# Running sums of exponentials over eight key tiles instead of two or four, in a fused attention and FFN block

## The chip, the cores and the metric

The kernel runs on one core of a Trainium2 chip. The metric is the device time of one execution in microseconds (us); before the change it is 3277.49 us, the median of three runs from 3269.68 to 3278.75. Five engines work side by side, each through its own queue in program order: TensorE (PE in the profile; its weight loads are PEld), VectorE (DVE), ScalarE (ACT), GpSimd (POOL) and SyncE (SP), which issues most of the transfers. ScalarE's queue issues some too.

## The reference

One pre-norm transformer block in float32, on x of 2 x 1024 x 1024 (batch, tokens, features), with 32 heads of 32 features and an FFN of 2752 hidden units:

```python
def attention(x):
    qkv = (x @ attn_qkvw + attn_qkvb).reshape(B, S, 3, HEADS, hd)
    q, k, v = (transpose(qkv[:, :, i], (0, 2, 1, 3)) for i in range(3))
    probs = softmax(einsum('bhqd,bhkd->bhqk', q, k) / sqrt(hd))
    ctx = transpose(einsum('bhqk,bhkd->bhqd', probs, v), (0, 2, 1, 3))
    return ctx.reshape(B, S, H) @ attn_ow + attn_ob

x = x + attention(layernorm(x))
h = layernorm(x)
x = x + (silu(h @ W_gate.T) * (h @ W_up.T)) @ W_down.T
```

## The kernel before

**Blocks, phases and units.** The tokens are taken in four blocks of 512 queries (two batches of two). A phase is the attention of one block; it has 16 units, and a unit is two heads against all 1024 keys, in NT = 8 key tiles of 128. So there are 64 units, of which the first 16 (phase 0) stand among the projections of batch 0, and those of phases 1 to 3 largely among the output projection and FFN of the block before. The FFN of the last block has no attention beside it. The FFN products are of Strassen's kind, with sums of weights prepared by GpSimd during phase 0 (`weight_sum_steps`, L1148).

**A unit, step by step.** `scores` (L500) takes two key tiles at once: eight 32-row products (recorded as 8 instructions for a pair of tiles) into two PSUM buffers; ScalarE copies each to a tile p of 128x1024 in SBUF (L528), VectorE keeps a running maximum over the tiles (L525). After the last pair the maximum over the keys is found and negated, goes out to HBM and comes back as a tile m, spread over all partitions. `less_maximum` (L579) adds m to each p, on GpSimd (in phase 0 every fourth tile on VectorE), and puts the exponential (L590, ScalarE) and the sum (L601) off to later. `values` (L610) multiplies p by v into one PSUM bank `acc`: 16 records in four column groups for each key tile, and 8 more records with a tile of ones wherever `summed(kt)` says that p holds a sum, which gives the denominators.

**Sums in place of separate products.** If p1 is replaced by p0 + p1, then p0 v0 + p1 v1 = p0 (v0 - v1) + (p0 + p1) v1, so the values stay right when v0 becomes v0 - v1, and the ones need to be multiplied with the sum only. `add` (L601) makes the sums, `differences` (L593) changes v. In phases 1 to 3 the sums go over two tiles (adds for kt = 1, 3, 5, 7; GpSimd does 1 and 5, VectorE 3 and 7), so ones are multiplied four times per unit; in phase 0 they go over four tiles (six adds by VectorE), so ones are multiplied twice.

**What sets the order.** All instructions are emitted by hand. An `Emitter` keeps a planned clock, which advances by a cost for each TensorE step (855 ns for a product of 512 columns, MM4). It merges two lists: `fill` (projections, FFN) and `paced` (attention), whose beats are spread evenly over the costs of the list; there is one beat for each key tile n of all units. `em.later(delay, fn)` puts a step off by so many ns of the planned clock. A step with `needs` waits in its list until another one has given that name. In each round n of `attention_steps` (L650) come, in this order: q and k loads of the next unit, the load of v (L493, at kt = 6), the scores (at even n), `less_maximum` of tile n - 11, and every fourth round a run of four `values`, for tiles up to n - 14. The tiles p lie in a ring of 19 (`RING`, L165), vals in two buffers.

**Block changes.** When a block's attention is complete, its ctx is loaded, multiplied by the reciprocals of the sums (`prep_ctx`, L697; the products are on GpSimd, L730, and wait for the tile rec), and the next output projection begins (L752), with bias sums on GpSimd (L774).

Of the kernel before, what the change touches and what calls it, by code (L numbers as in the profile page):

```python
# [12 lines left out]
ALU = mybir.AluOpType  # L13
# [117 lines left out]
def preln_block_kernel(  # L131
# [31 lines left out]
    LAG = 3  # L163
    RUN = 4
    RING = NT + LAG + RUN + 4  # L165

    const = ctx.enter_context(tc.tile_pool(name="const", bufs=1))
    lin = ctx.enter_context(tc.tile_pool(name="lin", bufs=1))
# [295 lines left out]
    class Unit:  # L464
# [35 lines left out]
        def scores(self, i):  # L500

            kts = (2 * i, 2 * i + 1)
            ps = [
                psum.tile([P, S], F32, tag="s", bufs=2, name=f"s_{self.name}_{kt}") for kt in kts
            ]
            for a in range(2):
                for h in range(2):
                    rows = slice((2 * a + h) * HD, (2 * a + h + 1) * HD)
                    nc.tensor.matmul(  # L509
                        ps[a][:, h * NH : (h + 1) * NH],  # L510
                        self.k[rows, i * P : (i + 1) * P],
                        self.q[rows, :],
                        start=True,
                        stop=True,
                    )


            for kt in kts:
                self.p[kt] = Pt(f"p_{self.name}_{kt}")

            def largest(kt, s):
                if kt == 1:
                    self.top = att.tile([P, S], F32, tag="top", bufs=1, name=f"top_{self.name}")
                if kt > 0:
                    nc.vector.tensor_tensor(self.top, s, self.p[0] if kt == 1 else self.top, ALU.max)  # L525

            def keep(kt, s):
                nc.scalar.copy(self.p[kt], s)  # L528

            if i == 0:  # L530
                keep(0, ps[0])
                em.later(2600.0, lambda: largest(1, ps[1]))
            else:
                largest(kts[0], ps[0])
                em.later(1600.0, lambda: keep(kts[0], ps[0]))
                em.later(1700.0, lambda: largest(kts[1], ps[1]))
            em.later(3300.0 if i > 0 else 4200.0, lambda: keep(kts[1], ps[1]))
            if kts[1] == NT - 1:
                self.maximum()
# [39 lines left out]
        def less_maximum(self, kt):  # L579
            p = self.p[kt]  # L580
            eng = nc.vector if self.phase == 0 and kt % 4 == 3 else nc.gpsimd
            eng.tensor_tensor(p, p, self.m, ALU.add)  # L582
            em.later(3500.0, lambda: self.exponential(kt))
            if kt % 2 == 1:
                twice = self.phase == 0 and kt % 4 == 3
                em.later(8100.0, lambda: self.add(kt, 1), None if twice else ("added", self.n, kt))
                if twice:
                    em.later(9900.0, lambda: self.add(kt, 2), ("added", self.n, kt))

        def exponential(self, kt):  # L590
            nc.scalar.activation(self.p[kt], self.p[kt], AF.Exp, scale=SCALE)  # L591

        def differences(self):  # L593

            v = self.v.rearrange("p (i a) n -> p i a n", a=2)
            nc.gpsimd.tensor_tensor(v[:, :, 0, :], v[:, :, 0, :], v[:, :, 1, :], ALU.subtract)
            if self.phase == 0:
                v = self.v.rearrange("p (i a) n -> p i a n", a=4)
                nc.gpsimd.tensor_tensor(v[:, :, 1, :], v[:, :, 1, :], v[:, :, 3, :], ALU.subtract)

        def add(self, kt, back):  # L601


            eng = nc.vector if self.phase == 0 or kt % RUN == RUN - 1 else nc.gpsimd
            eng.tensor_tensor(self.p[kt], self.p[kt], self.p[kt - back], ALU.add)  # L605

        def summed(self, kt):
            return kt % (4 if self.phase == 0 else 2) == (3 if self.phase == 0 else 1)

        def values(self, kt):  # L610

# [38 lines left out]
    def attention_steps(cuts):  # L650
# [10 lines left out]

        for i in range(2):
            load_step(0, i)
        for n in range(total + NT + LAG + 3):
            if n in cuts:
                q = Steps()
                lists.append(q)
# [1 line left out]
            if n < total:  # L669
                if kt == 1 or kt == 3:  # L670
                    load_step(k + 1, kt // 2)
                if n == 0:
                    q.add(lambda: em.later(9000.0, lambda: None, ("first",)))
                    q.add(lambda: None, needs=("first",))
                if kt == NT - 2:
                    q.add(units[k].load_v, needs=("v", units[k].b, units[k].hf))
            if n < total and kt % 2 == 0:
                q.add(lambda k=k, i=kt // 2: units[k].scores(i), MM4, beat=True)
            else:
                q.add(lambda: None, beat=True)  # L680
            k, kt = divmod(n - NT - LAG, NT)
            if 0 <= k < len(units):
                if kt == 0:
                    q.add(units[k].differences)
                q.add(lambda k=k, kt=kt: units[k].less_maximum(kt), needs=("max", k))
            k, kt = divmod(n - NT - LAG - 3, NT)
            if 0 <= k < len(units) and kt % RUN == RUN - 1:
                q.add(lambda: None, needs=("added", k, kt))
                for v in range(kt - RUN + 1, kt + 1):
                    cost = MM4 / 2 * (1 + units[k].summed(v))  # L690
                    q.add(lambda k=k, v=v: units[k].values(v), cost)
        return lists


# [660 lines left out]
```

## Time and profile before

| | before |
|---|---|
| median of three runs | 3277.49 us (3269.68 to 3278.75) |
| the profiled execution | 3264.24 us, span 3262.5 us, TensorE clock 0.996 |
| first and last score maximum of a unit (L567) | 123 us, 2712 us |
| first and last copy of a finished unit (L639) | 200.6 us, 2776.9 us |
| ScalarE busy: exponentials (L591), copies of scores (L528) | 533.2 us, 516.7 us |
| GpSimd busy: differences of v (L596, L599) | 56.3 us, 10.1 us |
| SP waiting for values before it loads v (L495) | 241.5 us, 57 times |

The units follow one another about every 41 us. A row of groups reads: line, engine, operation, what it writes and reads, shapes and count; then busy time in us and the mean of one in ns; then the engine's idle time just ahead of these instructions and what ended most of it. A float32 product is recorded as two instructions. A row of stages has the window, its length, and busy us and instruction counts of PE, PEld, DVE, ACT and POOL, followed by the granted clock, the share of the DMA engines and GB/s. A row of the timeline has start, length, engine, line and operation, with several like instructions merged.

### The profile page before, as it was taken

The numbers are of one execution on the slowest core, as the hardware profiler recorded it, in microseconds if no ns is written. First come the engines' busy times: TensorE is split into PE (matmuls) and PEld (weight loads), VectorE is DVE, ScalarE is ACT, GpSimd is POOL, SyncE is SP. The second block draws the span as 40 slices with busy tenths as digits, with TensorE's granted clock in tenths as the row PEclk, the third lists the DMA queues.
The fourth block names the chain that finished last, engine by engine and source line by source line (L and its number), as shares of the span: only waits on it lengthen the run. The fifth ranks groups of instructions, "written<-read, shape, count | busy, mean of one in ns | idle before, by whom it ended". The sixth has DMA issues, their size and how long they took to land.

```text
span 3262.5 us, 43853 instructions
## 1 busy us (share of the span) xinstructions
PE 3206.8 (98%) x16256; PEld 1792.5 (55%) x16256; DVE 1999.2 (61%) x2733; ACT 1432.7 (44%) x1570; POOL 1767.8 (54%) x871
## 2 busy tenths in 40 slices
PE   8999999999999999999999999999999999999999
PEld 4444444444346565663466555634666567477775
DVE  2266676666356677667766777676677774344334
ACT  2244554444456555554565555545655554010000
POOL 0267766776676555667766665667756555200000
PEclk9999999999999999999999999999999999999999
DMA  4566666655435444446344444463444444544442
GB/s 155 170 183 197 219 197 205 194 173 170 140 107 149 146 147 148 146 149 205 104 142 146 146 143 143 143 201 101 142 147 149 144 139 139 178 156 152 154 153 96
DMA packets 337828, 507.31 MB, mean 155 GB/s; under 512 B 105424, under 2 KB 122064, under 8 KB 337616
## 3 DMA queue, kind: packets, MB, share of 16 engines
q1 hardware_dynamic: 281424, 405.91, 39.9%
q10 hardware_dynamic: 56192, 98.60, 9.8%
q8 instruction: 130, 2.13, 0.3%
q14 instruction: 82, 0.67, 0.1%
HBM read 429.14 MB, written 75.24 MB: 155 GB/s over the span
## 4 chain that ended last, share of the span: by engine, by line
PE 86%; DVE 6%; DMA 3%; POOL 2%; issue 1%; ACT 1%; SPq 0%; ACTq 0%; POOLq 0%; DVEq 0%
PE p L924 31%; PE pq L370 11%; PE pd L1073 11%; PE acc L620 9%; PE s L509 7%; PE pvv L432 7%; PE po L782 7%; DVE top L525 1%; DVE x L1086 1%; POOL p L582 1%; DMA ctx<-dctx 1%; DMA rec<-drec 1%; PE pg L968 1%; PE pd L1000 1%; DVE p L605 1%
## 5 line engine op out<-in xcount | busy, mean ns | idle before, releaser
L582 POOL TENSOR_TENSOR p<-p,m 128x1024 f32<-128x1024 f32 x480 | 1193.3, 2508 | 11.5 <-DVE top L525 8.4
L528 ACT COPY p<-s 128x1024 f32<-128x1024 f32 x512 | 516.7, 1011 | 840.3 <-DVE top L525 642.1
L591 ACT ACTIVATE p<-p 128x1024 f32<-128x1024 f32 x512 | 533.2, 1057 | 270.0 <-POOL p L582 246.2
L525 DVE TENSOR_TENSOR top<-s,top 128x1024 f32<-128x1024 f32 x384 | 468.0, 1219 | 275.1 <-PE s L509 266.1
L924 PE MATMUL p<-sum,m 128*128 128x256 f32 x2688 | 616.7, 383 | 4.1 <-DVE sum L906 3.6
L924 PEld LDWEIGHTS p<-sum,m 128*128 128x128 f32 x2688 | 503.0, 190 | 126.5 <-issue 45.7
L605 POOL TENSOR_TENSOR p<-p,p 128x1024 f32<-128x1024 f32 x96 | 227.1, 2366 | 629.7 <-ACT p L591 595.6
L924 PE MATMUL p<-xn2T,m 128*128 128x256 f32 x2016 | 471.1, 383 | 5.2 <-DVE sum L833 2.4
L370 PE MATMUL pq<-xnT,wqk 128*128 128x512 f32 x1024 | 463.2, 601 | 0.0
L1073 PE MATMUL pd<-wp,h 128*128 128x512 f32 x960 | 438.0, 602 | 10.3 <-DVE x L1086 9.9
L924 PEld LDWEIGHTS p<-xn2T,m 128*128 128x128 f32 x2016 | 376.7, 190 | 104.4 <-issue 47.9
L605 DVE TENSOR_TENSOR p<-p,p 128x1024 f32<-128x1024 f32 x192 | 335.7, 1748 | 135.5 <-ACT p L591 134.8
L370 PEld LDWEIGHTS pq<-xnT,wqk 128*128 128x128 f32 x1024 | 188.2, 190 | 255.9 <-issue 252.7
L1073 PEld LDWEIGHTS pd<-wp,h 128*128 128x128 f32 x960 | 177.1, 190 | 248.1 <-issue 200.0
L509 PE MATMUL s<-q,k 32*128 32x512 f32 x2048 | 302.2, 643 | 10.6 <-ACT p L528 10.5
L1086 DVE TENSOR_TENSOR x<-pd,x 128x512 f32<-128x512 f32 x360 | 236.7, 681 | 71.1 <-PE pd L1073 70.6
L620 PE MATMUL acc<-p,vals 128*32 128x256 f32 x4096 | 266.2, 382 | 5.5 <-DVE p L605 5.4
L1186 POOL TENSOR_TENSOR ws<-raw 128x512 f32<-128x512 f32 x62 | 89.3, 1440 | 300.5 <-DMA raw<-in_w_gu 188.9
L432 PE MATMUL pvv<-wv,xnT 128*128 128x512 f32 x512 | 234.3, 603 | 2.4 <-ACT xnT L266 2.4
L782 PE MATMUL po<-wo,ctx 128*128 128x512 f32 x512 | 234.4, 608 | 0.0
L620 PEld LDWEIGHTS acc<-p,vals 128*32 128x32 f32 x4096 | 119.5, 109 | 147.3 <-issue 71.3
L952 ACT ACTIVATE gate<-gate 128x512 f32<-128x512 f32 x84 | 52.9, 630 | 278.0 <-DVE gate L951 277.4
(94 smaller groups left out, 2476.9 us busy)
## 6 DMA issues: line engine op xcount, KB each, us to landing
m<-dws SPq DMA_DIRECT2D x336, 256.0 KB
m<-in_w_gu SPq DMA_DIRECT2D x252, 256.0 KB
wp<-ddn SPq DMA_DIRECT2D x160, 256.0 KB
m<-d SPq DMA_DIRECT2D x64, 512.0 KB
wp<-in_w_dn SPq DMA_DIRECT2D x120, 256.0 KB
raw<-in_w_gu ACTq DMA_DIRECT2D x84, 256.0 KB
dws<-ws ACTq DMA_DIRECT2D x84, 256.0 KB
x<-in_x SPq DMA_DIRECT2D x32, 512.0 KB
```

The lines of the kernel that those rows point to most:

```text
L370: nc.tensor.matmul(ps, wqk[b, g, w, hk][:, k, :], xnT[b, s][:, kc, :], start=(kc == 0), stop=(kc == KC - 1),)
L432: nc.tensor.matmul(st["ps"], xnT[b, t // TB][:, kc, (t % TB) * P : (t % TB + 1) * P], st["w"][kc], start=(kc == 0), stop=(kc == KC - 1),)
L509: nc.tensor.matmul(ps[a][:, h * NH : (h + 1) * NH], self.k[rows, i * P : (i + 1) * P], self.q[rows, :], start=True, stop=True,)
L525: nc.vector.tensor_tensor(self.top, s, self.p[0] if kt == 1 else self.top, ALU.max)
L528: nc.scalar.copy(self.p[kt], s)
L582: eng.tensor_tensor(p, p, self.m, ALU.add)
L591: nc.scalar.activation(self.p[kt], self.p[kt], AF.Exp, scale=SCALE)
L605: eng.tensor_tensor(self.p[kt], self.p[kt], self.p[kt - back], ALU.add)
L620: nc.tensor.matmul(self.acc[j * HD : (j + 1) * HD, c : c + NQ], w(h), self.p[kt][:, q0 : q0 + NQ], start=start, stop=stop, skip_group_chec ...
L782: nc.tensor.matmul(st["ps"], ctxT[b, blk][:, g, t * P : (t + 1) * P], st["w"][hf, g], start=(g == 0), stop=(g == G - 1),)
L924: nc.tensor.matmul(ps, mats[c, n][:, kc, :], rhs, start=(kc == 0), stop=(kc == hk - 1),)
L1073: nc.tensor.matmul(st["pd"], lefts[n](pi)[:, j, t * P : (t + 1) * P], st["wp", pi, n, j], start=(j == 0), stop=(j == PART // 2 - 1),)
```

## The change

Four things change.

1. **Sums over all eight tiles, in all phases** (`SUMS = 8`). p of tile kt becomes the sum of the exponentials of tiles 0 to kt, in seven adds one after another. `summed` is true for kt = 7 alone, so ones are multiplied once per unit. `differences` makes seven instructions, v of tile a less v of tile a + 1.
2. **Who adds.** In phase 0 VectorE does all seven; in phases 1 to 3 VectorE does kt = 3, 5 and 7, GpSimd kt = 1, 2, 4 and 6. The adds are put off by 8100 ns (phase 0), 11000 ns (GpSimd) or 12500 ns (VectorE) of the planned clock after the tile's `less_maximum`, and by 500 ns again for as long as the add before has not been emitted.
3. **Values one tile later.** A run of four values is for tiles up to n - 15 instead of n - 14, and is emitted directly after the scores of the round and ahead of `less_maximum`, where before it came last in a round without scores. v is loaded one tile later (kt = 7).
4. **Tiles p are claimed when the scores are copied**, not when the score products are emitted. The ring keeps its 19 tiles.

```diff
+    SUMS = 8
...
-            for kt in kts:
-                self.p[kt] = Pt(f"p_{self.name}_{kt}")
...
             def keep(kt, s):
+
+                self.p[kt] = Pt(f"p_{self.name}_{kt}")
                 nc.scalar.copy(self.p[kt], s)
...
-            if kt % 2 == 1:
-                twice = self.phase == 0 and kt % 4 == 3
-                em.later(8100.0, lambda: self.add(kt, 1), None if twice else ("added", self.n, kt))
-                if twice:
-                    em.later(9900.0, lambda: self.add(kt, 2), ("added", self.n, kt))
+            if kt % SUMS > 0:
+
+                vec = self.phase == 0 or (kt > 1 and kt % 2 == 1)
+                delay = 8100.0 if self.phase == 0 else 12500.0 if vec else 11000.0
+                eng = nc.vector if vec else nc.gpsimd
+                em.later(delay, lambda: self.add(kt, eng))
...
-            v = self.v.rearrange("p (i a) n -> p i a n", a=2)
-            nc.gpsimd.tensor_tensor(v[:, :, 0, :], v[:, :, 0, :], v[:, :, 1, :], ALU.subtract)
-            if self.phase == 0:
-                v = self.v.rearrange("p (i a) n -> p i a n", a=4)
-                nc.gpsimd.tensor_tensor(v[:, :, 1, :], v[:, :, 1, :], v[:, :, 3, :], ALU.subtract)
-
-        def add(self, kt, back):
-
-
-            eng = nc.vector if self.phase == 0 or kt % RUN == RUN - 1 else nc.gpsimd
-            eng.tensor_tensor(self.p[kt], self.p[kt], self.p[kt - back], ALU.add)
+            v = self.v.rearrange("p (i a) n -> p i a n", a=SUMS)
+            for a in range(SUMS - 1):
+                nc.gpsimd.tensor_tensor(v[:, :, a, :], v[:, :, a, :], v[:, :, a + 1, :], ALU.subtract)
+
+        def add(self, kt, eng):
+
+            if kt % SUMS > 1 and ("added", self.n, kt - 1) not in em.done:
+                em.later(500.0, lambda: self.add(kt, eng))
+                return
+            eng.tensor_tensor(self.p[kt], self.p[kt], self.p[kt - 1], ALU.add)
+            em.done.add(("added", self.n, kt))

         def summed(self, kt):
-            return kt % (4 if self.phase == 0 else 2) == (3 if self.phase == 0 else 1)
+            return kt % SUMS == SUMS - 1
...
-        for n in range(total + NT + LAG + 3):
+        for n in range(total + NT + LAG + 4):
...
-                if kt == NT - 2:
+                if kt == NT - 1:
                     q.add(units[k].load_v, needs=("v", units[k].b, units[k].hf))
...
+
+            k, kt = divmod(n - NT - LAG - 4, NT)
+            if 0 <= k < len(units) and kt % RUN == RUN - 1:
+                q.add(lambda: None, needs=("added", k, kt))
+                for v in range(kt - RUN + 1, kt + 1):
+                    cost = MM4 / 2 * (1 + units[k].summed(v))
+                    q.add(lambda k=k, v=v: units[k].values(v), cost)
             k, kt = divmod(n - NT - LAG, NT)
             if 0 <= k < len(units):
                 if kt == 0:
                     q.add(units[k].differences)
                 q.add(lambda k=k, kt=kt: units[k].less_maximum(kt), needs=("max", k))
-            k, kt = divmod(n - NT - LAG - 3, NT)
-            if 0 <= k < len(units) and kt % RUN == RUN - 1:
-                q.add(lambda: None, needs=("added", k, kt))
-                for v in range(kt - RUN + 1, kt + 1):
-                    cost = MM4 / 2 * (1 + units[k].summed(v))
-                    q.add(lambda k=k, v=v: units[k].values(v), cost)
```

## The prediction

> **What bounds the kernel now.** I read the engine shares first, then the groups by line and shape, then the busy time by stage, then single moments on the timeline.
>
> ```profile
> PE 3206.8 (98%) x16256; PEld 1792.5 (55%) x16256; DVE 1999.2 (61%) x2733; ACT 1432.7 (44%) x1570; POOL 1767.8 (54%) x871
> ```
>
> TensorE is busy 98% of the span at a granted clock of 0.996, and the chain of waits gives it 86%. So removed TensorE work shortens the span unless something new makes TensorE wait. The attention rows, from the groups by line:
>
> ```profile
> L620 PE MATMUL acc<-p,vals 128*32 128x256 f32 x4096 | 266.2, 382 | 5.5 <-DVE p L605 5.4
> L620 PE MATMUL acc<-p,ones 128*32 128x256 f32 x1792 | 138.4, 381 | 0.0
> L605 DVE TENSOR_TENSOR p<-p,p 128x1024 f32<-128x1024 f32 x192 | 335.7, 1748 | 135.5 <-ACT p L591 134.8
> L605 POOL TENSOR_TENSOR p<-p,p 128x1024 f32<-128x1024 f32 x96 | 227.1, 2366 | 629.7 <-ACT p L591 595.6
> L582 POOL TENSOR_TENSOR p<-p,m 128x1024 f32<-128x1024 f32 x480 | 1193.3, 2508 | 11.5 <-DVE top L525 8.4
> ```
>
> The products with ones (row sums of the exponentials) are what the change thins out; the adds at L605 are what it pays with. POOL idles 630 us ahead of its 96 adds, waiting for ScalarE: it runs ahead and has slack. How much depends on the stage (busy us of PE, PEld, DVE, ACT, POOL):
>
> ```profile
> 1000.00:1500.00 500.00, 495.76 (x2934) 309.31 (x2932) 346.50 (x498) 267.90 (x283) 298.78 (x137) 1.00 0.48 148
> 1500.00:1620.00 120.00, 117.54 (x591) 49.98 (x592) 85.41 (x104) 63.33 (x68) 98.83 (x48) 0.97 0.50 155
> 2090.00:2240.00 150.00, 142.06 (x712) 64.61 (x711) 104.69 (x126) 68.13 (x70) 108.61 (x57) 0.97 0.54 165
> ```
>
> In a steady FFN stage POOL is busy 60% and TensorE loses 1%; where one block's FFN gives way to the next block's output projection POOL is busy 72 to 82% and TensorE loses 2 to 5%.
>
> **Products with ones, removed.** Before, units of phase 0 sum twice per eight tiles, units of phases 1 to 3 four times; afterwards every unit once. That is 16 x 1 + 48 x 3 = 160 groups of 8 records gone (1280 of 1792). Price of a group, from TensorE's timeline (start, length):
>
> ```profile
> 1575.15 0.59 PE L782 MATMUL po<-wo,ctx 128*128 128x512 f32 x1
> 1575.67 1.07 PE L620 MATMUL acc<-p,vals 128*32 128x256 f32 x16
> 1576.56 0.61 PE L620 MATMUL acc<-p,ones 128*32 128x256 f32 x8
> 1576.99 1.05 PE L620 MATMUL acc<-p,vals 128*32 128x256 f32 x16
> 1577.86 0.61 PE L620 MATMUL acc<-p,ones 128*32 128x256 f32 x8
> 1578.40 0.70 PE L782 MATMUL po<-wo,ctx 128*128 128x512 f32 x1
> ```
>
> From the start of ones to the next start is 0.43 us (1576.56 to 1576.99). The group row would say 138.4/1792 x 8 = 0.62 us, but its busy time holds the overlapping ends; I take starts: 160 x 0.43 = **-69 us** (-99 by the row).
>
> **Value runs put behind score products.** Before, scores (32*128 tiles) and values (128*32 tiles) are separate visits between 128*128 products. From the rows above a visit of values enters 0.52 - 0.44 = 0.08 us late (a projection product lasts 0.44) and leaves 0.54 - 0.43 = 0.11 late; a score visit in the same timeline (1570.97 to the next projection at 1572.04, for 0.88 of streaming) leaves 0.19 late and enters about as the other. [...] by the rows alone between nothing and a whole exit and entry (0.27 us, -35). I take -15.
>
> **POOL.** In phases 1 to 3 a unit has four POOL adds where it had two: +2 x 2.36 = 4.7 us. The differences of v, one instruction of 128x256 (median 730 ns), become seven of 128x64. The rows at 128x256 and 128x128 (457 ns) extrapolate to 0.32 us, so 2.3, and 2.6 with a short semaphore wait each; bounds 1.9 and 7 x 0.73 = 5.1. So +1.9. Per unit in the steady stage POOL goes from 298.8/12 = 24.9 us to 31.5; adding 1.5 for standing behind VectorE gives 33.0 of a period of 41.7 - 1.3 - 0.2 = 40.2 us: 82%. Still below TensorE, with 7 us of slack per unit instead of 17. In phase 0 POOL gains 1.4 us per unit over its 71%; its weight sums wait for transfers anyway. I cost that at nothing; if the cover is gone it is at most 16 x 1.4 = 22 us.
>
> **VectorE.** A unit has three adds instead of two in phases 1 to 3, seven instead of six in phase 0: +64. Both inputs lie in SBUF, where POOL reads too:
>
> ```profile
> 1993.76 2.81 POOL L582 TENSOR_TENSOR p<-p,m 128x1024 f32<-128x1024 f32 x1
> 1994.27 3.38 DVE L605 TENSOR_TENSOR p<-p,p 128x1024 f32<-128x1024 f32 x1
> 1995.03 1.56 PE L924 MATMUL p<-xn2T,m 128*128 128x256 f32 x6
> 1996.43 1.89 PE L924 MATMUL p<-sum,m 128*128 128x256 f32 x8
> ```
>
> An add of 1.23 us (median) took 3.38 because it met a POOL instruction, and TensorE ran on. [...] with POOL at 82% in runs of two or three instructions, an add would stand behind a whole run (two or three times 2.36 us), 6 to 8 us with 1.23 of its own, three times a unit: VectorE would go from 28.9 to above 43.6 us per unit and become the bound: 48 x (43.6 - 40.2) = 163 us, and a clear loss. The trace shows that only twice (6.88 us at 1570.06, 6.90); the other slow adds end within 3.4 us, that is after one POOL instruction, whose successor then takes 3.36. So I take 2.3 us for an add: VectorE 28.9 + 3 x 2.3 - 2 x 1.63 = 32.5 us of 40.2, 81%. TensorE waits for L605 for 13 us in the whole trace, nearly all in the two dense windows; in steady stages one slow add is followed by a pause of TensorE (0.5 us at 1008), the others by none. What pauses there are (19 us in 1430) follow other VectorE instructions with two SBUF inputs (L906, L954, L1048) which POOL holds up; with POOL a third busier I add **+6 us**.
>
> **The chain of adds.** It now alternates: POOL 1, 2, VectorE 3, POOL 4, VectorE 5, POOL 6, VectorE 7. Behind a waiting POOL add stand the next subtractions of the maximum, so ScalarE's exponentials; behind a waiting VectorE add stand PSUM evictions and score maxima, so TensorE's next banks. By the planner's own clock the last add of a run is issued 3.4 to 5.8 us ahead of its values (before: 6 to 7 in most units of phases 1 to 3). The same distance, 3.8 to 4.3, stood in phase 0 before, where TensorE waited 1.1 us for adds in 750 us. Allowed: **+5 us**. In phase 0 the distance grows to 9; nothing. Moving load_v by one tile and its wait on SP (already 241.5 us for values, ahead of weight loads) moves with the value runs, one tile apart as before; the p tiles, claimed at the copy, keep their ring of 19. No cost for either.
>
> **Block changes.** At about 850 to 930, 1478 to 1580 and 2127 to 2225 us POOL is full: ctx products wait for rec (98.8 us over all blocks), bias sums follow. There 2.5 units bring 2.5 x 6.6 = 16.5 us more, of which I let some 5 be absorbed: 3 x 11 = **+33 us**. Bounds 0 and 3 x 24 (all of it, and half as much again for TensorE's evictions).
>
> **Sum:** -69 - 15 + 6 + 5 + 33 = -40 us. Against the profiled execution's 3264.24 that is 3224; the runs shown have a median of 3277.49, 13 higher, so I predict **3237 us**.
>
> **Rivals.** *All of the gain arrives* (0.20): POOL's slack takes the block changes too; -84, 3193. For it: POOL idles 630 us ahead of its adds. Against: the two dense windows lose time already.
> *Swallowed* (0.15): block changes cost their upper bound, 72, with 11 elsewhere: -84 + 83, about 3277.
> *Slower* (0.20): POOL becomes the bound. A unit costs it 24.9 + 2.3 (other work, 110/48) + 2.1 (rec waits) = 29.3 us; add 4.7, differences at 0.5 each 2.8, 3 x 1.0 behind VectorE's adds, and 2 x 1.5 waiting for VectorE in the alternation: 42.8, over the 41.2 us that a unit takes now (47 units from 842 to 2777). That costs 48 x 1.6 = 77: about 3354. It decides once POOL's unit passes 41 us. Against: 82% by the rows.
> The forecast itself has 0.45, with 3210 to 3265 as its own range.
>
> **Numbers.** A measurement of this kernel can tell 0.3% (10 us) from no change. Faster: 0.20, plus nearly all of 0.45: 0.63. Same 0.15; slower 0.22. The range runs from the full gain to the foot of the slower case, 3190 to 3300.
>
> **What would show it.** Ones x512 at 0.43 us per group; POOL 78 to 86% busy in steady FFN stages and over 90% at block changes; VectorE adds at 2 to 2.6 us mean; TensorE's pauses grown mainly at the three block changes; 128x64 differences at 0.3 to 0.4 us. It is wrong if POOL's idle time ahead of its adds vanishes in the steady stages, if adds of 6 us become common, or if TensorE waits for L605's adds in every unit.

## The result, and the profile after

| | before | after |
|---|---|---|
| median | 3269.38 us (3264.63 to 3278.75, 20 runs) | 3279.26 us (3275.81 to 3288.5, 20 runs) |
| ratio to before | | **1.0031**, 95% interval 1.0023 to 1.0038 |
| profiled execution | 3264.24 us | 3280.72 us |
| its span, TensorE clock | 3262.5 us, 0.996 | 3279.0 us, 0.986 |

The changed kernel is 10 us slower by the medians, where 3237 was predicted: a gain of 40 on the 3277 known then, for a loss of 10 on 3269. (The profiled executions differ by 16.5 us, as that of before lies 5 us under its median and that of after 1.5 over; what follows splits these two.) TensorE's work did shrink, from 16256 records to 14976 and by 50 us of busy time. Yet the span is longer.

```profile
PE 3157.1 (96%) x14976; PEld 1770.8 (54%) x14976; DVE 2131.9 (65%) x2797; ACT 1429.2 (44%) x1569; POOL 2164.7 (66%) x1335
```

The groups by line and shape answer to the rows of before (lines have moved: L620 is now L622, L605 is L606, L582 is L583, L591 is L593):

```profile
L622 PE MATMUL acc<-p,vals 128*32 128x256 f32 x4096 | 261.3, 396 | 10.6 <-DVE p L606 10.6
L622 PE MATMUL acc<-p,ones 128*32 128x256 f32 x512 | 39.9, 384 | 0.0
L606 DVE TENSOR_TENSOR p<-p,p 128x1024 f32<-128x1024 f32 x256 | 444.1, 1735 | 134.3 <-ACT p L593 76.4 <-POOL p L606 57.7
L606 POOL TENSOR_TENSOR p<-p,p 128x1024 f32<-128x1024 f32 x192 | 474.6, 2472 | 287.4 <-DVE p L606 200.9 <-ACT p L593 77.5 <-ACT gate L939 8.8
L583 POOL TENSOR_TENSOR p<-p,m 128x1024 f32<-128x1024 f32 x480 | 1214.6, 2544 | 2.8 <-DMA m<-d 2.8
L599 POOL TENSOR_TENSOR vals<-vals 128x64 f32<-128x64 f32 x448 | 196.2, 438 | 30.1
```

Ones fell to 512 records. GpSimd's idle time ahead of its adds, the slack that the prediction counted on, fell from 630 to 287 us, and over two thirds of what is left is waiting for VectorE's adds. The stages (busy us of PE, PEld, DVE, ACT, POOL, then the granted clock, DMA share and GB/s) show the rest:

```profile
1000.00:1500.00 500.00, 487.57 (x2693) 308.55 (x2692) 379.39 (x523) 274.96 (x292) 398.05 (x237) 1.00 0.51 152
1500.00:1620.00 120.00, 107.12 (x487) 44.51 (x484) 77.94 (x87) 55.90 (x60) 110.76 (x69) 0.94 0.43 134
2090.00:2240.00 150.00, 138.14 (x656) 68.12 (x656) 98.28 (x125) 67.97 (x71) 124.32 (x78) 0.94 0.53 157
```

In the steady stage TensorE is busy 97.5% where it had 99%. At the block changes it loses 8 to 11%, and the granted clock goes to 0.94. GpSimd is at 80% in the first row and 92% in the second.

**Where the time went.** I split each span in three, from the trace. *Pauses* are gaps of over 20 ns between TensorE's matmuls. *Half rate* is the loss in stretches in which the record of the granted clock stands at 0.5: half of their length, without the part that is a pause already (in one of 3.5 us TensorE has 4 records of products, in the 3.4 us after it 9: last section). *Work* is what remains.

| us | span | pauses | half rate (stretches) | work |
|---|---|---|---|---|
| before | 3262.5 | 44.1 | 13.4 (6) | 3205.0 |
| after | 3279.0 | 109.9 | 39.9 (18) | 3129.1 |
| difference | +16.5 | +65.8 | +26.5 | -75.9 |

So 76 us of work were saved and 92 us were given back. The pauses by region: 160 to 880 us (phase 0) 4.0 before and 12.6 after; the steady stages (960 to 1480, 1640 to 2140, 2260 to 2800) 20.8 and 53.8; the three block changes around them 16.9 and 41.2.

**Who TensorE waited for.** The waits of before, then of after (engine, what it would write and line, what it waited for; us in total, times, longest):

```profile
ACT p L591 <- POOL p L582: 246.2, 98, 11.4
PE s L509 <- ACT p L528: 10.5, 5, 3.9
PE pd L1073 <- DVE x L1086: 9.9, 13, 1.9
PE p L924 <- ACT gate L936: 2.3, 3, 1.2
```

```profile
ACT p L593 <- POOL p L583: 474.4, 169, 11.7
PE s L510 <- ACT p L529: 36.9, 19, 6.9
PE pd L1076 <- DVE x L1089: 29.7, 28, 3.2
PE p L927 <- ACT gate L939: 8.8, 5, 3.5
```

Little of it is waiting for the sums themselves (10.6 us; 5.4 before). TensorE waits for PSUM banks that ScalarE (score copies, gate copies) and VectorE (x, the FFN's output) have not emptied in time.

To see why they were late, each pause can be followed back through the trace: from the instruction that ended it through its engine's queue for as long as that engine was busy, then to what that engine had waited for, and so on for 15 us or until TensorE is reached. This gives three kinds (us of pauses):

| | through GpSimd | VectorE adds in the chain, no GpSimd | neither |
|---|---|---|---|
| steady stages, before | 0.0 | 4.8 | 16.0 |
| steady stages, after | 9.9 | 27.3 | 16.5 |
| block changes, before | 6.2 | 4.7 | 6.0 |
| block changes, after | 29.2 | 0.0 | 12.0 |

In the steady stages most of the growth (22 of 33 us) has VectorE's own adds in the chain. An example from VectorE's queue in the kernel after (start, length, engine, line):

```profile
2500.35 1.22 DVE L606 TENSOR_TENSOR p<-p,p 128x1024 f32<-128x1024 f32 x1
2501.48 2.83 DVE L1051 TENSOR_TENSOR h<-h 128x512 f32<-128x512 f32 x1
2504.24 2.47 DVE L1089 TENSOR_TENSOR x<-pd,x 128x512 f32<-128x512 f32 x4
```

The add and a sum of h stand ahead of the four evictions of x, so TensorE stops for 1.83 us for a bank (its rows are under "What the hardware showed", where VectorE is busy 13.40 of 13.50 us). A chain that holds an add does not prove that the add made it late, but the experiments below bear the kinds out.

The other 10 us in the steady stages, and most at the block changes, come through GpSimd: ScalarE's exponentials wait 474 us for GpSimd's subtractions where they waited 246 before. One moment on the timeline shows the path from there to TensorE (in brackets the idle time before and its releaser):

```profile
1887.77 3.71 POOL L599 TENSOR_TENSOR vals<-vals 128x64 f32<-128x64 f32 x7
...
1891.43 2.34 POOL L583 TENSOR_TENSOR p<-p,m 128x1024 f32<-128x1024 f32 x1
...
1893.81 1.06 ACT L593 ACTIVATE p<-p 128x1024 f32<-128x1024 f32 x1 [4.89 <-POOL p L583]
1894.88 1.28 ACT L955 ACT_TABLE_LOAD   x1
...
1896.18 0.63 ACT L955 ACTIVATE gate<-gate 128x512 f32<-128x512 f32 x1
...
1896.84 2.11 DVE L957 TENSOR_TENSOR h<-gate,up 128x512 f32<-128x512 f32 x1 [4.43 <-ACT gate L955]
1898.88 2.54 DVE L524 TENSOR_TENSOR top<-s,top 128x1024 f32<-128x1024 f32 x2
1900.12 1.01 ACT L529 COPY p<-s 128x1024 f32<-128x1024 f32 x1 [3.31 <-DVE top L524]
1901.03 0.38 ACT L939 COPY gate<-p 128x256 f32<-128x256 f32 x1
...
1901.46 4.72 PE L927 MATMUL p<-sum,m 128*128 128x256 f32 x13 [3.06 <-ACT gate L939]
```

The seven differences hold GpSimd for 3.7 us, so the next subtraction is late. The exponential that needs it stands in ScalarE's queue ahead of the FFN's activation (L955) and of the 1.28 us in which ScalarE loads the table for it; VectorE waits 4.4 us for that, its score maxima come late, so do ScalarE's score copy and the gate copy behind it, and TensorE stops for 3.06 us. No engine is full over the whole stage. Each queue passes on the lateness of another.

### The profile page after: what moved, and what is told of

Its sections match the earlier page's. It is cut to its first block, busy times and chain, and to the rows that moved or that the text cites. A ratio compares the mean times of both kernels' runs of the same rounds, so it can differ in the third digit from the quotient of the medians.

```text
span 3279.0 us, 42344 instructions
## 1 busy us (share of the span) xinstructions
PE 3157.1 (96%) x14976; PEld 1770.8 (54%) x14976; DVE 2131.9 (65%) x2797; ACT 1429.2 (44%) x1569; POOL 2164.7 (66%) x1335
## 4 chain that ended last, share of the span: by engine, by line
PE 49%; DVE 9%; POOL 5%; ACT 2%; issue 2%; DMA 1%; SPq 0%; ACTq 0%; POOLq 0%; DVEq 0%
PE p L927 27%; PE pd L1076 9%; PE acc L622 4%; PE s L510 4%; POOL p L583 3%; PE po L785 3%; DVE x L1089 2%; DVE top L524 2%; DVE p L606 1%; PE pg L971 1%; PE pd L1003 1%; POOL vals L599 1%; ACT p L529 1%; POOL p L606 1%; DVE h L957 1%
## 5 line engine op out<-in xcount | busy, mean ns | idle before, releaser
L583 POOL TENSOR_TENSOR p<-p,m 128x1024 f32<-128x1024 f32 x480 | 1214.6, 2544 | 2.8 <-DMA m<-d 2.8
L593 ACT ACTIVATE p<-p 128x1024 f32<-128x1024 f32 x512 | 533.2, 1057 | 532.9 <-POOL p L583 474.4
L606 POOL TENSOR_TENSOR p<-p,p 128x1024 f32<-128x1024 f32 x192 | 474.6, 2472 | 287.4 <-DVE p L606 200.9
L606 DVE TENSOR_TENSOR p<-p,p 128x1024 f32<-128x1024 f32 x256 | 444.1, 1735 | 134.3 <-ACT p L593 76.4
L1076 PE MATMUL pd<-wp,h 128*128 128x512 f32 x960 | 440.9, 606 | 28.5 <-DVE x L1089 28.4
L510 PE MATMUL s<-q,k 32*128 32x512 f32 x2048 | 321.9, 657 | 36.9 <-ACT p L529 36.9
L1076 PEld LDWEIGHTS pd<-wp,h 128*128 128x128 f32 x960 | 178.9, 192 | 269.8 <-issue 197.2
L1189 POOL TENSOR_TENSOR ws<-raw 128x512 f32<-128x512 f32 x62 | 97.0, 1565 | 274.2 <-DMA raw<-in_w_gu 173.1
L622 PE MATMUL acc<-p,vals 128*32 128x256 f32 x4096 | 261.3, 396 | 10.6 <-DVE p L606 10.6
L622 PEld LDWEIGHTS acc<-p,vals 128*32 128x32 f32 x4096 | 122.3, 113 | 187.7 <-issue 91.3
L599 POOL TENSOR_TENSOR vals<-vals 128x64 f32<-128x64 f32 x448 | 196.2, 438 | 30.1
```

The source lines that it names most:

```text
L510: nc.tensor.matmul(ps[a][:, h * NH : (h + 1) * NH], self.k[rows, i * P : (i + 1) * P], self.q[rows, :], start=True, stop=True,)
L606: eng.tensor_tensor(self.p[kt], self.p[kt], self.p[kt - 1], ALU.add)
L622: nc.tensor.matmul(self.acc[j * HD : (j + 1) * HD, c : c + NQ], w(h), self.p[kt][:, q0 : q0 + NQ], start=start, stop=stop, skip_group_chec ...
L1076: nc.tensor.matmul(st["pd"], lefts[n](pi)[:, j, t * P : (t + 1) * P], st["wp", pi, n, j], start=(j == 0), stop=(j == PART // 2 - 1),)
```

## The experiments

All times are medians; the ratio to before with its interval is the measure between kernels. "Steady" is the busy share of VectorE and GpSimd in the three steady windows (1000 to 1500, 1620 to 2090, 2240 to 2700 us); the last three columns are the split of the span, as above, for the one profiled execution of each kernel, which for some is several us from the median.

| run | time | ratio [95%] | steady VectorE, GpSimd | pauses | half rate | work |
|---|---|---|---|---|---|---|
| before | 3269.38 | | 70%, 61% | 44.1 | 13.4 | 3205.0 |
| after | 3279.26 | 1.0031 [1.0023, 1.0038] | 76%, 81% | 109.9 | 39.9 | 3129.1 |
| e1_order | 3261.15 | 0.9979 [0.9972, 0.9986] | 68%, 62% | 66.9 | 16.0 | 3181.5 |
| e2_pool_adds | 3255.47 | 0.996 [0.9948, 0.9972] | 63%, 73% | 39.9 | 18.0 | 3195.4 |
| e3_dve_adds | 3349.2 | 1.0253 [1.0235, 1.0271] | 85%, 61% | 163.1 | 53.0 | 3142.5 |
| e4_one_diff | 3249.42 | 0.9939 [0.9926, 0.9952] | 77%, 78% | 89.5 | 38.5 | 3124.0 |
| e5_one_handover | 3299.59 | 1.0096 [1.0083, 1.0109] | 77%, 80% | 132.2 | 41.4 | 3129.1 |
| e6_no_pool_adds | 3237.59 | 0.9906 [0.9893, 0.992] | 75%, 69% | 82.7 | 27.0 | 3122.0 |
| e7_no_dve_add | 3250.02 | 0.9943 [0.9929, 0.9956] | 73%, 80% | 90.9 | 31.7 | 3122.0 |
| e8_sums_of_4 | 3284.57 | 1.0049 [1.0035, 1.0062] | 74%, 77% | 89.9 | 36.5 | 3139.6 |
| e9_order_ctx_later | 3262.16 | 0.9988 [0.9979, 0.9996] | 68%, 62% | 63.6 | 13.5 | 3183.4 |
| e10_after_ctx_later | 3275.32 | 1.0022 [1.0014, 1.0029] | 76%, 82% | 106.6 | 35.2 | 3124.4 |
| e11_one_diff_ctx_later | 3252.48 | 0.9953 [0.9941, 0.9965] | 77%, 79% | 102.4 | 27.4 | 3122.9 |
| e12_five_pool_adds | 3265.79 | 1.0011 [0.9995, 1.0028] | 73%, 82% | 113.9 | 34.8 | 3124.6 |
| e13_order_ctx_later_2 | 3248.37 | 0.9936 [0.992, 0.9952] | 68%, 62% | 49.6 | 16.1 | 3181.8 |
| e14_one_diff_ctx_later_2 | 3242.14 | 0.9915 [0.9901, 0.993] | 77%, 79% | 86.1 | 29.2 | 3120.8 |

### The parts alone: order, and who adds

**e1_order** is the kernel before with the new order of value runs alone:

```diff
+            k, kt = divmod(n - NT - LAG - 4, NT)
...
             k, kt = divmod(n - NT - LAG, NT)
...
-            k, kt = divmod(n - NT - LAG - 3, NT)
```

(with load_v at NT - 1 and the tiles claimed at the copy, as in the change).

> The kernel before, with only the new order: runs of values one tile later and directly behind the score products, v loaded one tile later, tiles p claimed at the copy. Sums and adds as before. Theory A (GpSimd is too full, and what waits for it pauses TensorE) and rival B (the alternation of adds between GpSimd and VectorE pauses it) both expect the saved mode change alone: 128 runs x 0.093 us = 12 us less than before, about 3257 us, pauses of TensorE near 44 us and a granted clock near 0.996. Rival C (the new order itself makes score products wait for ScalarE's copies) expects 20 us or more of further pauses and a time at or above before's 3269.

Measured 3261: 7 us faster. The order saves 23.5 us of work, more than the 12 us of the "mode change", as joining a score visit and a value run is called in that expectation (0.093 us a run, measured below), but adds 23 us of pauses, nearly all at block changes. The two longest stand at 1514 and 2170 us. The first on the timeline of e1_order:

```profile
1516.15 1.26 POOL L728 TENSOR_TENSOR ctx<-ctx,rec 128x512 f32<-128x512 f32 x1 [12.92 <-DMA rec<-drec]
...
1519.43 2.34 POOL L580 TENSOR_TENSOR p<-p,m 128x1024 f32<-128x1024 f32 x1
...
1521.80 1.06 ACT L589 ACTIVATE p<-p 128x1024 f32<-128x1024 f32 x1 [15.50 <-POOL p L580]
...
1522.89 2.94 DVE L603 TENSOR_TENSOR p<-p,p 128x1024 f32<-128x1024 f32 x1 [10.63 <-ACT p L589]
...
1525.76 1.87 DVE L1009 TENSOR_TENSOR x<-pd,x 128x512 f32<-128x512 f32 x3
1526.49 1.22 PE L998 MATMUL pd<-wd,h 128*128 128x512 f32 x1 [12.23 <-DVE x L1009]
```

GpSimd stands 12.9 us at a ctx product for a transfer (rec). Behind it in turn stand subtractions, exponentials, a VectorE add, evictions, and TensorE. That the wait is there because values one tile later let a block's last unit end later, while the ctx products keep their due time, is my reading; e13 below puts the due time off.

**e2_pool_adds** moves the 96 VectorE adds of phases 1 to 3 to GpSimd, in the kernel before. **e3_dve_adds** moves the 192 GpSimd adds to VectorE, in the kernel after.

```diff
-            eng = nc.vector if self.phase == 0 or kt % RUN == RUN - 1 else nc.gpsimd
+            eng = nc.vector if self.phase == 0 else nc.gpsimd
```

```diff
-                vec = self.phase == 0 or (kt > 1 and kt % 2 == 1)
-                delay = 8100.0 if self.phase == 0 else 12500.0 if vec else 11000.0
+                vec, delay = True, 8100.0
```

> The kernel before, with the two adds per unit that VectorE makes in phases 1 to 3 given to GpSimd: +2 x 2.36 us per unit on GpSimd (about 71% busy in steady stages instead of 60%), VectorE eased, products with ones and order as before, no alternation. Theory A expects TensorE's pauses to grow by 20 to 40 us and the clock to fall below 0.993: 3290 to 3320 us. Rival B expects no change, 3260 to 3278.

> The changed kernel, with all seven adds on VectorE in all phases (8100 ns after the subtraction, as in phase 0): GpSimd loses 4 x 2.4 us per unit and the alternation is gone. A and B both expect pauses back near 44 us, clock near 0.995 and most of the 81 us of saved TensorE work kept: 3195 to 3220 us. If VectorE (73 to 78% busy in steady stages, now some 85 to 90%) takes over as the cause of pauses, the time stays above 3250.

They go opposite ways, and theory A is wrong on both, B on e3, where the third reading (over 3250) came true: e2 is 13 us faster than before, e3 70 us slower than after. Steady-stage sums of e2_pool_adds, then of e3_dve_adds:

```profile
sum 1430.00, PE 1416.25 PEld 891.80 DVE 899.89 ACT 792.38 POOL 1043.75; mean PE 472.08 PEld 297.27 DVE 299.96 ACT 264.13 POOL 347.92
```

```profile
sum 1430.00, PE 1328.05 PEld 807.30 DVE 1211.74 ACT 747.62 POOL 866.11; mean PE 442.68 PEld 269.10 DVE 403.91 ACT 249.21 POOL 288.70
```

And TensorE's main wait in e3_dve_adds, from its groups:

```profile
L1075 PE MATMUL pd<-wp,h 128*128 128x512 f32 x960 | 448.9, 612 | 53.8 <-DVE x L1088 52.7 <-DVE gate L949 0.8
```

In e2 GpSimd is at 73% and TensorE pauses less than before. In e3 GpSimd is back at 61%, VectorE at 85% empties the x banks late, and pauses reach 163 us. In the steady stages e2, where VectorE makes no adds, has 9.8 us of pauses; e3 has 118.9, of which 113.7 with an add in the chain. So a fuller GpSimd cost nothing where VectorE was relieved for it, and a fuller VectorE cost much although GpSimd was relieved. (e3 also puts all its adds off by 8100 ns instead of 11000 or 12500; what that does alone was not run.)

### One cost taken away at a time

**e4_one_diff**: one instruction in place of seven differences.

```diff
-            for a in range(SUMS - 1):
-                nc.gpsimd.tensor_tensor(v[:, :, a, :], v[:, :, a, :], v[:, :, a + 1, :], ALU.subtract)
+            nc.gpsimd.tensor_tensor(v[:, :, : SUMS - 1, :], v[:, :, : SUMS - 1, :], v[:, :, 1:, :], ALU.subtract)
```

> The changed kernel, with the seven subtractions of v made by one instruction of 128x448 (about 1.1 us for 7 x 0.44): 2 us per unit less on GpSimd, alternation untouched. Theory A expects a third of the added pauses and clock loss back: 3245 to 3265 us. Rival B expects the changed kernel's time within 5 us, 3274 to 3284.

```profile
L598 POOL TENSOR_TENSOR vals<-vals 128x448 f32<-128x448 f32 x64 | 91.5, 1430 | 0.0
```

The row of e4_one_diff has 1.43 us per unit for 7 x 438 ns = 3.07 us. This 1.6 us (105 us of GpSimd busy time in all) made the kernel 30 us faster, with pauses 20 us shorter. In the steady stages the pauses through GpSimd fell from 9.9 to 3.4 us, while those with VectorE adds stayed at 27.2.

**e5_one_handover**: the same four GpSimd and three VectorE adds per unit, in the order GpSimd 1 to 4, VectorE 5 to 7, so one handover in place of five.

```diff
-                vec = self.phase == 0 or (kt > 1 and kt % 2 == 1)
+                vec = self.phase == 0 or kt > 4
```

> The changed kernel, with the adds of phases 1 to 3 dealt out in two blocks: GpSimd makes 1 to 4, VectorE 5 to 7. As many adds on each engine, but one handover per unit in place of five. Rival B (the alternation pauses TensorE; GpSimd waits 201 us for VectorE's adds) expects pauses down from 110 to 80 us or less and 3250 us or less. Theory A (GpSimd too full) and theory D (each add on VectorE, which also empties the PSUM banks, costs TensorE) expect the changed kernel's 3279 within 6 us.

20 us slower than after, which neither side expected. Fewer handovers alone don't bring the time back; what a handover costs can't be read from this run, as it has a new cost of its own: three VectorE adds in a row stand ahead of the evictions, and TensorE's products pd (L1076) wait 47.6 us for x instead of 29.7.

**e6_no_pool_adds** leaves out GpSimd's adds for kt = 2 and 4, **e7_no_dve_add** VectorE's for kt = 5, both in phases 1 to 3.

```diff
+            if self.phase == 0 or kt not in (2, 4):
                 eng.tensor_tensor(self.p[kt], self.p[kt], self.p[kt - 1], ALU.add)
```

```diff
+            if self.phase == 0 or kt != 5:
                 eng.tensor_tensor(self.p[kt], self.p[kt], self.p[kt - 1], ALU.add)
```

> The changed kernel, leaving out GpSimd's adds of tiles 2 and 4 in phases 1 to 3, so that the sums there are not the reference's. GpSimd is left with the two adds per unit that it had before the change; VectorE keeps three. A expects GpSimd down by 4.7 us per unit and most of the added pauses and half-rate stretches gone: 3215 to 3240 us. D expects little, 3265 to 3280.

> The changed kernel, leaving out VectorE's add of tile 5 in phases 1 to 3, so that the sums there are not the reference's. VectorE is left with the two adds per unit that it had before, GpSimd keeps four. D (with 13 us for 96 adds, from the kernel before with its adds moved to GpSimd) expects 7 to 15 us less than the changed kernel: 3264 to 3272. A expects under 5 us. B expects more, 3255 or less, as GpSimd's add of tile 6 no longer waits for VectorE.

96 GpSimd adds fewer give 42 us, 48 VectorE adds fewer give 29. That is 0.43 us of time per GpSimd add of 2.47, and 0.6 per VectorE add of 1.74. e6 came out where A had it; e7 is at 3250, far below D's range, where B had it. Leaving an add out also cuts the chain that the others wait in: GpSimd's wait for VectorE's adds falls from 200.9 to 112.6 us in e6 and to 184.7 in e7. So these two runs don't separate an engine's time from the chain. In the steady stages the pauses with VectorE adds fell from 27.3 to 15.8 (e6) and 18.0 us (e7), those through GpSimd from 9.9 to 1.1 and 4.7. Both resources were priced too low; neither alone explains the loss.

**e8_sums_of_4** is e4 with sums over four tiles and two VectorE adds per unit in phases 1 to 3:

```diff
-    SUMS = 8
+    SUMS = 4
...
-                vec = self.phase == 0 or (kt > 1 and kt % 2 == 1)
+                vec = self.phase == 0 or kt % SUMS == SUMS - 1
```

> The changed kernel's order and its differences in one instruction, but sums over four tiles in all phases: GpSimd adds tiles 1, 2, 5, 6 and VectorE 3 and 7 in phases 1 to 3 (GpSimd as many adds as in the changed kernel, VectorE as many as before), ones twice per unit. Against the changed kernel with differences in one instruction (3249 us) TensorE works 64 x 0.43 = 28 us more. A alone expects 3249 + 28 = 3277 less the saved half-rate time of nothing, so 3265 to 3280. D and B expect VectorE's third add and the long chain to be what pauses TensorE: pauses near 50 us and half-rate loss near 15, 3215 to 3245 us, below both kernels.

3285, 5 us above A's range and 40 above that of D and B, with runs from 3268 to 3305. The profiled execution is the fastest of these, so its split stands for that one alone. In it the pauses are as long as e4's, with shorter chains and a VectorE add less per unit, and TensorE waited 20 us for the sums (16.2 for VectorE's adds, 3.9 for GpSimd's), where after has 10.6. So neither the number of VectorE's adds nor the length of the chain decides alone; what else makes it slow, and why its runs scatter so, is open.

### The block changes

**e9_order_ctx_later**, **e10_after_ctx_later** and **e11_one_diff_ctx_later** are e1, after and e4 with the ctx products due 7 us later, so that GpSimd doesn't stand waiting for rec:

```diff
-            em.later(5000.0, go, ("mult", b, blk, i))
-            em.later(8000.0, lambda: None, ("prep", b, blk, i))
+            em.later(12000.0, go, ("mult", b, blk, i))
+            em.later(15000.0, lambda: None, ("prep", b, blk, i))
```

> The kernel of e1 (before, with the new order alone), with the ctx products put off by 12000 instead of 5000 ns of the planned clock (and the name prep given at 15000 instead of 8000), so that GpSimd does not stand in its queue waiting for rec while subtractions, exponentials and VectorE's next add are behind it. If that wait is what the order costs (two pauses of 12.2 us at the block changes), those two pauses go and the time falls from 3261 to 3228 to 3242 us. If the pauses have another cause, 3255 or more.

> The changed kernel with the same later ctx products. Its block changes hold about 29 us of pauses, half of them in the chain behind GpSimd's wait for rec. Expected 10 to 25 us less than 3279 if the wait for rec counts here too; within 5 us if GpSimd's and VectorE's own work is all that counts.

> The changed kernel with the differences in one instruction (3249 us) and the later ctx products. If the two causes are separate, their gains add: 3225 to 3240 us, the fastest so far and below both kernels.

All three missed the gain that was hoped for; e9 and e11 lie within the noise of e1 and e4, and e10, 4 us under after, within its own second reading. By the rule set for e9 the pauses would have another cause; its trace says otherwise. In e9 the two pauses of 12 us are gone, but the gain was given back at the first block change, where TensorE waits for the products themselves:

```profile
926.27 4.63 PE L780 MATMUL po<-wo,ctx 128*128 128x512 f32 x5 [13.40 <-POOL ctx L728]
```

Pauses between 880 and 960 us went from 5.3 to 19.2 us in e9, from 9.0 to 18.2 in e10 and from 5.3 to 22.6 in e11; at the other two changes they went from 33.5 to 14.4 (e9 against e1). So **e13_order_ctx_later_2** and **e14_one_diff_ctx_later_2** are e9 and e11 with the later due times for all but the first block:

```diff
+            em.later(12000.0 if b + blk > 0 else 5000.0, go, ("mult", b, blk, i))
+            em.later(15000.0 if b + blk > 0 else 8000.0, lambda: None, ("prep", b, blk, i))
```

> The kernel of e9, with the first block's ctx products left at 5000 ns; only the later blocks' are put off. In e9 the pauses of 12 us at the second and third block change went, but TensorE waited 13.4 us for the ctx products at the first. If the wait for rec behind GpSimd is what the order costs at the block changes, pauses fall from e1's 67 to about 45 and the time to 3240 to 3252. If it stays at 3258 or more, the loss at block changes has another cause.

> The changed kernel with the differences in one instruction (e4, 3249 us), later ctx products for all blocks but the first. If the block-change part adds to the part in the steady stages: 3228 to 3243 us, below every kernel so far. If the steady stages alone count: 3245 to 3253.

Both came out as expected. e13 is 13 us faster than e1 and pauses 17 us less: the two long pauses were the order's lost gain. e14 is 7 us faster than e4, and with 3242 us (0.9915 [0.9901, 0.993]) the fastest kernel here that computes the whole reference; it beats both before and after.

**e12_five_pool_adds** is e11 with five GpSimd and two VectorE adds per unit:

```diff
-                vec = self.phase == 0 or (kt > 1 and kt % 2 == 1)
+                vec = self.phase == 0 or kt % 4 == 3
```

> The kernel of e11, with the add of tile 5 moved from VectorE to GpSimd in phases 1 to 3 (GpSimd 1, 2, 4, 5, 6; VectorE 3, 7). By the rates seen so far, an add less on VectorE gains some 29 us (e7) and an add more on GpSimd costs some 21 us (half of e6): about 8 us less than e11. If GpSimd (near 80% busy) has passed the point where it bounds the unit, 10 us or more above e11.

3266, 13 us slower than e11 by the medians (runs from 3258 to 3287), as its second reading had it. But the profiled execution, 9 us above the median, doesn't show GpSimd as the bound: it is at 82%, and the pauses through it in the steady stages are 8.3 us for 7.0. One pause stands out:

```profile
2617.43 13.62 DVE L956 TENSOR_TENSOR h<-gate,up 128x512 f32<-128x512 f32 x1 [3.34 <-ACT gate L954]
2630.97 1.21 DVE L605 TENSOR_TENSOR p<-p,p 128x1024 f32<-128x1024 f32 x1
...
2632.23 1.08 PE L621 MATMUL acc<-p,vals 128*32 128x256 f32 x8 [12.22 <-DVE p L605]
```

A product of h, 0.69 us at its shortest, took 13.6 us while GpSimd ran six instructions, four subtractions and two adds, without a gap from 2616.63 to 2630.50. The add behind it was late and TensorE stopped for 12.2 us; in the profiled executions that is all of the 11.5 us by which e12's pauses exceed e11's. Whether it is so in every run is open.

### What the runs say together

Put in order of VectorE's steady share, the pauses follow: 40 to 67 us at 63 to 70% (e2, e13, e9, e1, before), 83 to 132 at 73 to 77% (after and the rest), 163 at 85% (e3). The steady stages alone give the same groups: 10 to 21, 32 to 54 (e5 78) and 119 us. Within the middle group GpSimd's share goes along with the pauses: 83 at 69% (e6), 86 to 102 at 77 to 80% (e8, e14, e4, e7, e11), 107 to 114 at 81 and 82% (e10, after, e12), with e5 (132 at 80%) above. So both engines count; in e3 VectorE alone is enough, with GpSimd at its old 61%. This is an order among kernels that differ in more than one thing, no test of either share. Nor does it separate the length of the chain: every kernel of the middle group has sums over eight or four tiles in phases 1 to 3, and none has long sums with a VectorE at 65%. How much of the step from 60 to 85 us is the chain and how much VectorE's share is open.

## Why the prediction was wrong

**Right: the work.** Ones went to 512 records. TensorE's start times give the prices (medians): before, a score visit takes 1.164 us and a value run of phases 1 to 3 with its two groups of ones 2.821. Joined they take 3.028 in the run without ones and 3.460 in the run with one group. That is 0.957 or 0.525 us less per run, of which ones are 0.864 or 0.432, and 0.093 is what joining a score visit and a value run saves. That was put at 0.115, the author's estimate: a quarter of the 0.46 us by which, in the prediction's rows, the two visits enter and leave late (0.08 + 0.11 and 0.08 + 0.19). So 128 runs come to 12 us for 15, and the ones to the 69. The sum of 81 stands against 76 in the split of the span, but the parts agree less: e1's order alone saved 23.5 us of work, and the sums over eight tiles 52.4 more. Why is open.

**Right: the shares.** GpSimd in steady stages was put at 82% and is at 81%, VectorE at 81% and is at 76%. A VectorE add takes 1.735 us, below the 2.3 assumed. The case priced at 163 us, adds that stand behind a whole run of GpSimd instructions, came up for one add of 256 (4.87 us, at two subtractions; no other took over 3.4); the last section has the few other cases. 128x64 differences have the estimated median of 319 ns, but a mean of 438 in their chain, so 3.07 us per unit for 2.6.

**Right in size by luck: the block changes**, +24 us of pauses for +33. The prediction put them on the work that GpSimd gets more there. But the order alone (e1), with no add or difference more, already has +22: GpSimd stands at the ctx products for rec. After the whole change GpSimd is in most of these chains too, with its differences and adds in them: e4's single difference takes 9 us off the three changes, e10's later products 6 off the second and third. The two causes do not add up, and how they share the 24 us is open.

**Wrong: the pauses of the steady stages and of phase 0.** The steps "+6 us" (evictions held up) and "+5 us" (the chain of adds), and phase 0 "at nothing", come to 11; measured are +33 in the steady stages and +9 in phase 0 (of which 4 come with the order alone). Two things were mis-sized in the steady stages. The larger is VectorE. The paragraph on the chain did say that PSUM evictions stand behind an add; but as nearly all slow adds before had left TensorE running, the +6 was meant for other instructions, and a third add per unit got no more than its share of the +5. Pauses with adds in the chain grew by 22 us. The smaller was put at nothing: GpSimd late, exponentials late, ScalarE's queue with its activations and copies behind them, VectorE, TensorE, 10 us. The prediction named its first half, the subtractions and exponentials behind a waiting GpSimd add, and priced only the wait for the sums.

**Wrong: the sum lacks a term.** Pauses were followed by stretches at half rate, 6 in the kernel before and 18 after. That added 26.5 us, and nothing stood for it in "-69 - 15 + 6 + 5 + 33 = -40". With +41 for the +11, +24 for the +33, -76 for the -84 and +26.5 the sum is +16, the measured difference of the spans. None of the prediction's own signs of being wrong came up: GpSimd kept idle time ahead of its adds, adds of 6 us did not occur, and TensorE waited for an add only 9 times. They watched the adds, and the loss showed in the evictions. Of the signs that were to show it, two failed: the adds' mean of 2 to 2.6 us, and pauses that grow mainly at the block changes (24 us there, 33 in the steady stages).

**The rivals.** *Swallowed* (3277) came closest, but by another road: the block changes did not cost 72. In *slower*, GpSimd was to become the bound; busy 81% of the steady stages it did not, and the loss came before that point. *All of the gain* had for it GpSimd's 630 us of idle time ahead of its adds; as 342 us of it went, ScalarE's exponentials waited 228 us longer for subtractions.

## What to carry to other kernels

When work moves from the bounding engine to two helpers, price the lateness that passes from queue to queue, not only their busy share. Begin with what stands behind the new work in the helper's own queue: here evictions behind VectorE's adds, 22 us. Then list what stands in the queue of the engine that the helper feeds, up to the bank that the bounding engine needs next: here exponentials, activations and copies behind GpSimd, 10 us. A little helper time can be worth much: 1.6 us of GpSimd time per unit were worth 30 us of 3279 while no helper was over 81% busy in the steady stages. And a pause of TensorE can cost more than its length (here 26.5 us of half rate came with 65.8 us of added pauses), so short ones are worth removing too. A single step that waits for a transfer, in a queue that others depend on, may be put off until the transfer is sure to have landed (e13: 13 us faster than e1), but not where the bounding engine has nothing else to do (e9: TensorE stood 13.40 us).

## What the hardware showed

**Short pauses brought half rate.** TensorE around 2504 us in the kernel after, on the timeline:

```profile
2502.61 1.12 PE L1076 MATMUL pd<-wp,h 128*128 128x512 f32 x2
2505.57 7.10 PE L1076 MATMUL pd<-wp,h 128*128 128x512 f32 x12 [1.83 <-DVE x L1089]
```

and in three short windows there (columns as in the stages):

```profile
2492.00:2505.50 13.50, 11.74 (x65) 4.36 (x64) 13.40 (x15) 4.63 (x5) 12.37 (x11) 1.00 0.58 172
2505.50:2509.00 3.50, 3.44 (x4) 1.51 (x5) 3.50 (x6) 1.01 (x1) 3.50 (x3) 0.51 0.09 16
2509.00:2512.40 3.40, 3.40 (x9) 1.52 (x8) 1.86 (x3) 1.97 (x2) 2.85 (x2) 1.00 0.43 145
```

After a pause of 1.83 us the clock is 0.51 for 3.5 us: 4 records of products where the next 3.4 us have 9. In the kernel after there are 18 such stretches, of 3.41 us or two or three times that, and each follows pauses that add up to 1.1 to 3.4 us within the 3.41 us before it. It has 29 pauses of over 1.5 us for its 18 stretches; before has 9 for its 6. What tells the pauses apart is in the traces too: within a run all stretches start a whole number of 3.413 us apart. With the 16 traces cut into windows on that grid, from 20 us on, each of the 146 windows at full clock in which TensorE stood still for over 2.02 us was followed by half rate (5 of them in the kernel before, 12 in the kernel after), none of those with less than 0.81 us was, and in between 64 of 454 were (1 of 15 before, 6 of 41 after). So where a pause lies counts: in the kernel after, 2.50 us at 481 us lay across an edge (0.77 us before it, 1.73 after) and brought no half rate, the 1.83 us above lay inside one window and did. In the table of runs the loss is 0.2 to 0.45 us for each us of pause, and 26.5 for 65.8 between the two kernels.

**VectorE waited for one GpSimd instruction, or for a whole run of them.** The length of VectorE's adds did not follow GpSimd's share: in the steady stages their mean was 1.71 us before, with GpSimd at 61%, 1.66 after, with 81%, and 1.22 in e1, where the order had changed and GpSimd was at 62%. In e1 all but one of these adds began when no subtraction was running, and took 1.20 to 1.22 us; in the other two kernels, those that began during a subtraction took up to 3.38, about what is left of one GpSimd instruction and their own time. A few VectorE instructions with two SBUF inputs, none to three in each execution, were held for longer: the 13.6 us above, 7.20 us in the kernel after (a product of h at 2760 us, three GpSimd instructions), 6.88 and 6.90 before (adds, three), 9.25 in e1 (an add, five). Each of these ended 0.55 us (h) or 1.09 us (adds) after the run of GpSimd instructions, less than it takes alone (0.69 and 1.20). Why these waited for the whole run and the others for one instruction is open.
